# Row maxima turned in 32x32 blocks, context normalised on ScalarE, FFN work re-spaced

## The chip, the cores and the metric

The kernel runs on one core of one Trainium2 chip. The metric is the device time of one execution in microseconds (us): the median of several runs. PE is TensorE, PEld its weight loads, DVE VectorE, ACT ScalarE, POOL GpSimd; SP is SyncE, whose queue issues nearly all transfers (DMAs). A line number such as L836 is a line of the kernel before unless the text says that it is one of the changed kernel.

## What is computed

The input x is 32 sequences of 256 tokens with 128 features, float32. Three residual blocks follow each other:

```python
x = x + 0.5 * ffn(layernorm(x))          # "first FFN"
x = x + attention_block(layernorm(x))    # 16 heads of 8 features
x = x + 0.5 * ffn(layernorm(x))          # "second FFN"
```

The FFN has weights of +1 or -1, made from booleans: 128 to 512 with relu, 512 to 512 with relu, 512 to 128, each with a scale. The attention block projects to Q, K and V, takes a softmax over 256 keys for every head and query, multiplies by V, adds the block's input and ends in a layernorm with gamma and beta.

## The kernel before

**Tiling.** The 32 sequences are worked on as 16 units of two sequences (512 tokens, b = 0 and 1 inside a unit). Activations that enter matmuls are split into two float16 parts, a high one (h1h, h2h, qkhl row 0, xT row 0) and a low one that holds what rounding lost (h1l, h2l and so on), and each weight tile is multiplied with both.

**FFN.** `ffn` runs 4 products for the first layer, 16 for the second (4 outputs, each summed over 4 chunks) and 4 for the third. `dense` (L416) writes each product either as one matmul over all 128 columns of the array (L420, tiling D) or as four that each use 32 columns (L423, tiling C). `relu_split` follows each output: ACT makes the high part, DVE the low part (L664); by choice of the planner ACT instead writes a float32 copy (`full`, L666 or L667) from which POOL casts and subtracts (L661, L667).

**Attention.** For a unit and a sequence, `maxima` runs eight steps: PE makes the scores of two heads' groups (`nat`, L825, with 32 rows of the array each, called tiling R here), and DVE takes the maximum over the keys (`nm`, L836). `shift` turns these maxima into a row that is added to Q's extra rows, so that the second pass over the scores comes out shifted: ACT and POOL split nm into a high and a low float16 part (`mt`, L848 to L850), PE transposes mt into PSUM (`pm`, L855), ACT copies it to SBUF (`mr`, L860), one transfer takes mr to a DRAM tile (`dm`, L861), and another takes dm into the rows of Q (L862). `weigh` runs eight steps again: scores the other way round (`sc`, L895), exp on ACT (`pt`, L907), and products with V (`cx`, L877). `context` transposes cx back (`tp`, L921), divides by the sum of weights, adds the residual, normalises (`normalize`, tag "c") and applies gamma and beta. For all units but the last, `normalize` subtracts the mean and multiplies by the inverse deviation in two POOL operations (L617, L618).

**Order.** Nothing above is issued in the order of its text. Every operation is recorded with an engine, a cost, a due time (`rank`) and what it reads and writes; `_Plan.simulate` then lays all operations out on five engines, lowest rank first, with the buffers that are free, and `run` emits them in that order, which is then fixed on each engine. One step of `maxima` or `weigh` is one unit of rank, called a beat: 16 beats belong to a unit. The first maximum of unit u has rank 16u, and `weigh` follows `maxima` by BW = 13 beats, so that most beats hold one nat and one sc group, which use different rows of the array and are emitted interleaved. Products of the FFN, the projections and the transposes fill the array between the beats. Two PSUM tiles of the tag "sc" hold the scores of both passes, three of the tag "m" hold all other products, pm among them. The first FFN of unit u has due times from B0 + P0*u on (B0 = -30, P0 = 16.003); the second FFN of unit u from B1 + max(16u, 17.354 min(u, 1) + 16 max(u - 1, 0)) on, with B1 = 42.462. `relief` and `divert` in the planner decide, with the constants BIAS and BIAS2, which relu work goes to POOL.

Of the kernel before, what the change touches and what calls it, by code (L numbers as in the profile page):

```python
# [36 lines left out]
F32 = mybir.dt.float32  # L37
F16 = mybir.dt.float16
I32 = mybir.dt.int32
U8 = mybir.dt.uint8  # L40
AF = mybir.ActivationFunctionType
ALU = mybir.AluOpType
AX = mybir.AxisListType

P = 128
H = 16
HD = 8
G = 4
R = 4
EPS = 1e-5  # L50
# [6 lines left out]

QF, QK = 1, 1

QL = 1  # L60

UNIT = 16
B0, BA, BP, BW, BV, B1 = -30, -10.627, -6.547, 13, 4, 42.462

P0, P1, P2, SLOW = 16.003, 17.354, 16, 1

TURN_X, TURN_C = 1.5, 1.5  # L70

WARM = 14

BB = 15.813

RUSH, AHEAD = -0.12, 4.08

SKIP0, SKIP, UNTIL = 10.311, 2.868, 28.215

FAR = 19.64  # L80

HOLD = (0, 0.0, 0.0)

CAST = 1.0

WAIT = 0.057

KIND2 = 'F'

# [2 lines left out]

AFTER, REACH = (0.165, 0.085, 0.11, 0.04, 0.0), (0.053, 0.033, 0.037, 0.08, 0.05)

BIAS = 1.115

BIAS2 = 0.714
PE, DVE, ACT, POOL, SP = range(5)


# [19 lines left out]
class _Plan:  # L120
# [269 lines left out]
def tile_macaron(ctx: ExitStack, tc: tile.TileContext, x, Wq, bq, Wk, bk, Wv, bv, gamma, beta, k0, k1, k2, s0, s1, s2, out):  # L390
    nc = tc.nc
    plan = _Plan(tc)
    op = plan.op
    B, S, D = x.shape
    DFF = k1.shape[0]
    NF = DFF // P
    NU = B // 2
    TU = 2 * S
    NT = TU // P
# [33 lines left out]
    ident16 = const.tile([P, P], F16, name="ident16")  # L433
# [60 lines left out]
    scale = const.tile([P, 3], F32, name="scale")  # L494
# [5 lines left out]
    def projections():  # L500
# [89 lines left out]
    def normalize(dst, src, tag, n, rank, scale=1.0, quick=False):  # L590

        of = lambda: src[0].t[:, src[1] : src[1] + n]
        srcs = [(src[0], src[1] + t) for t in range(0, n, 2)]
        mv = buf(small, [P, n, 2], F32, f"mv{tag}", 4, f"mv_{tag}")
        ve = buf(small, [P, n], F32, f"ve{tag}", 4, f"ve_{tag}")
        rs = buf(small, [P, n, 1], F32, f"rs{tag}", 4, f"rs_{tag}")
        step = 2 if quick else n
        for a in range(0, n, step):
            part = slice(a, a + step)
            ts = range(a, a + step)  # L600
            for t in ts:
                st = buf(small, [P, 6], F32, f"st{tag}", 4, f"st_{tag}_{t}")
                op(DVE, 0.195, lambda t=t, st=st: nc.vector.bn_stats(st.t, of()[:, t, :]), r=[srcs[t // 2]], w=[st], rank=rank)
                op(DVE, 0.085, lambda t=t, st=st: nc.vector.bn_aggr(mv.t[:, t, :], st.t), r=[st], w=[(mv, t)], rank=rank)
            op(POOL, 0.27, lambda part=part: nc.gpsimd.tensor_scalar(ve.t[:, part], mv.t[:, part, 1], EPS, 1.0 / scale**2, ALU.add, ALU.mult),
               r=[(mv, t) for t in ts], w=[(ve, a)], rank=rank)
            op(POOL, 0.35 + 0.2 * step, lambda part=part: nc.gpsimd.tensor_tensor(rs.t[:, part, 0], ve.t[:, part], nhalf[:, part], ALU.pow),
               r=[(ve, a), "nhalf"], w=[(rs, a)], rank=rank)
        mvs = [(mv, t) for t in range(n)]
        if quick:  # L610
            for t in range(n):
                op(DVE, 0.26, lambda t=t: nc.vector.tensor_scalar(dst.t[:, t, :], of()[:, t, :], mv.t[:, t, 0:1], rs.t[:, t, :], ALU.subtract, ALU.mult),
                   r=[srcs[t // 2], (rs, t // 2 * 2), (mv, t)], w=[(dst, t)], rank=rank)
        else:
            dsts = [(dst, t) for t in range(n)]
            cost = 0.2 + 0.2 * n
            op(POOL, cost, lambda: nc.gpsimd.tensor_tensor(dst.t, of(), bc(mv.t[:, :, 0:1], D), ALU.subtract), r=[*srcs, *mvs], w=dsts, rank=rank)  # L617
            op(POOL, cost, lambda: nc.gpsimd.tensor_tensor(dst.t, dst.t, bc(rs.t, D), ALU.mult), r=[(rs, 0)], w=dsts, rank=rank)  # L618
# [19 lines left out]
    xs, xns, xTs, nms, cxs = {}, {}, {}, {}, {}  # L638
# [11 lines left out]
    def norm_ffn(key, src, n, rank, quick):  # L650
        name = f"{key[0][-1]}_{key[1]}_{key[-1]}"
        xn = buf(work, [P, n, D], F32, "fxn", 2, f"fxn{name}")
        normalize(xn, src, f"f{key[0][-1]}", n, rank, XS, quick)
        xTs[key] = turned(xn, key[0][-1], name, n, rank)
# [15 lines left out]
    def ffn(key, srcs, n, rank, span):  # L670
# [49 lines left out]
                0.1 + w / 455, lambda: nc.gpsimd.tensor_tensor(to(), to(), full.t.rearrange("p (t d) -> p t d", d=D), ALU.add)))  # L720
        return dsts

    def norm_first(u):
        norm_ffn(("ffn0", u), (xs[u], 0), NT, (B0 + P0 * u - AHEAD) if u >= QF else B0 - 0.5 + 2 * (u - 1) if u else -950, u < QF)

    def first(u):
        rank = B0 + P0 * u
        ffn(("ffn0", u), (xs[u], 0), NT, rank, P0)

    def second(u, b):  # L730
        n, part = (NT, 0) if b is None else (2, 2 * b)
# [2 lines left out]
        rank = at(u) + (b or 0) * UNIT / 2  # L734
        norm_ffn(("ffn1", u, b), (xs[u], part), n, rank - AHEAD, u >= NU - QL)
        dsts = ffn(("ffn1", u, b), (xs[u], part), n, rank, span * n / NT)
# [103 lines left out]
    def shift(u, b):  # L840

        rank = -1000
        nm, j = nms.pop((u, b)), u % NV
        Q = qs[j]
        nmr = [(nm, g, pr) for g in range(G) for pr in range(2)]
        ns = buf(small, [P, 2, R, G], F32, "ns", 4, f"ns_{u}_{b}")
        mt = buf(small, [P, 2, R, 2, G], F16, "mt", 4, f"mt_{u}_{b}")
        op(ACT, 0.2, lambda: nc.scalar.mul(mt.t[:, :, :, 0, :], nm.t, 1.0 / ONE), r=nmr, w=[(mt, 0)], rank=rank)  # L848
        op(POOL, 0.25, lambda: nc.gpsimd.tensor_scalar(ns.t, nm.t, 1.0 / ONE, None, ALU.mult), r=nmr, w=[ns], rank=rank)
        op(POOL, 0.3, lambda: nc.gpsimd.tensor_tensor(mt.t[:, :, :, 1, :], ns.t, mt.t[:, :, :, 0, :], ALU.subtract), r=[ns, (mt, 0)], w=[(mt, 1)], rank=rank)  # L850
        pm = psum([32, 2, P], f"pm_{u}_{b}", F16)

        def turn():
            for qc in range(2):
                nc.tensor.transpose(pm.t[:, qc, :], mt.t[:, qc].rearrange("p r l g -> p (r l g)"), ident16)  # L855

        op(PE, 0.12, turn, r=[(mt, 0), (mt, 1), "ident16"], w=[pm], rank=(u + 0.5 * b) * UNIT + 8.06, kind="C")
        mr = buf(small, [32, S], F16, "mr", 4, f"mr_{u}_{b}")
        dm = buf(dram, [32, S], F16, "dm", 4, f"dm_{u}_{b}")
        op(ACT, 0.25, lambda: nc.scalar.copy(mr.t, pm.t.rearrange("p q n -> p (q n)")), r=[pm], w=[mr], rank=rank)  # L860
        op(SP, 0.35, lambda: nc.sync.dma_start(out=dm.t, in_=mr.t), r=[mr], w=[dm], rank=rank, lag=1.4)  # L861
        op(SP, 0.63, lambda: nc.sync.dma_start(  # L862
            out=Q.rearrange("(x j) g n -> j x g n", j=16)[3][:, :, b * S : b * S + S],
            in_=dm.t.rearrange("(x g) n -> x g n", g=G)), r=[dm], w=[("S", j, b)], rank=rank, lag=1.8)

    def weigh(u, b):
        base = (u + 0.5 * b) * UNIT + BW
# [85 lines left out]
    for u in range(NU):  # L953
# [48 lines left out]
```

## Time and profile before

| | |
|---|---|
| three runs: median, lowest, highest | 688.74, 687.92, 688.95 us |
| the profiled execution's own time | 689.46 us |
| its span, first to last instruction | 687.6 us |
| mean granted clock of PE over the span | 0.995 |
| busy PE, DVE, ACT, POOL | 659.8, 581.1, 543.1, 497.3 us |
| DMA | 33.59 MB in 33391 packets |

The profile comes from one execution. Its span is 1.86 us shorter than that execution's time; those 1.86 us lie around the program's instructions. A row of a group names the line, the engine, what is written from what, the shape and the count, then busy time and mean duration of one, then the idle time of the engine before such instructions and who ended it. An engine's recorded durations overlap at their edges: DVE's sum to 656 us, of which 581.1 are distinct. Where the text says "exclusive", the time is meant that an instruction adds after the end of the one before it on its engine: 1158 ns for a maximum whose duration is 1216.

### The profile page before, as it was taken

The numbers are of one execution on the slowest core, as the hardware profiler recorded it, in microseconds if no ns is written. First come the engines' busy times: TensorE is split into PE (matmuls) and PEld (weight loads), VectorE is DVE, ScalarE is ACT, GpSimd is POOL, SyncE is SP. The second block draws the span as 40 slices with busy tenths as digits, with TensorE's granted clock in tenths as the row PEclk, the third lists the DMA queues.
The fourth block names the chain that finished last, engine by engine and source line by source line (L and its number), as shares of the span: only waits on it lengthen the run. The fifth ranks groups of instructions, "written<-read, shape, count | busy, mean of one in ns | idle before, by whom it ended". The sixth has DMA issues, their size and how long they took to land.

```text
span 687.6 us, 28926 instructions
## 1 busy us (share of the span) xinstructions
PE 659.8 (96%) x12596; PEld 344.6 (50%) x12596; DVE 581.1 (85%) x1194; ACT 543.1 (79%) x871; POOL 497.3 (72%) x685
## 2 busy tenths in 40 slices
PE   7998978999999999999999999999999999999996
PEld 4544533545455554555455454555445454544455
DVE  7789887998989798898979889897988888889484
ACT  3546887788889888888978888897889787868953
POOL 6875596688686868768686877868686785865643
PEclk9999998999999999999999999999999999999999
DMA  7222200203011030301102030200203021300000
GB/s 222 76 79 80 64 23 3 83 5 98 5 49 54 3 98 4 100 4 58 46 5 97 3 99 5 76 27 16 86 5 97 4 74 30 96 4 20 5 17 31
DMA packets 33391, 33.59 MB, mean 49 GB/s; under 512 B 4992, under 2 KB 29056, under 8 KB 33264
## 3 DMA queue, kind: packets, MB, share of 16 engines
q1 hardware_dynamic: 31520, 30.89, 14.3%
q8 instruction: 99, 1.62, 1.0%
q10 hardware_dynamic: 1744, 0.85, 0.4%
q14 instruction: 28, 0.23, 0.1%
HBM read 18.58 MB, written 13.14 MB: 46 GB/s over the span
## 4 chain that ended last, share of the span: by engine, by line
PE 82%; DVE 7%; ACT 4%; POOL 3%; DMA 2%; issue 1%; SPq 0%; ACTq 0%; POOLq 0%
PE p_None L423 18%; PE p L423 17%; PE cx L877 16%; PE sc L895 9%; PE p L420 6%; DVE nm L836 4%; PE p_None L420 3%; PE nat L825 3%; ACT pt L907 2%; PE tp L921 2%; PE pq L423 2%; PE pq L420 1%; PE pv L423 1%; PE t L630 1%; PE t_None L630 1%
## 5 line engine op out<-in xcount | busy, mean ns | idle before, releaser
L836 DVE TENSOR_REDUCE nm<-nat 128x4 f32<-128x1024 f32 x256 | 310.5, 1216 | 27.4 <-PE nat L825 22.0
L907 ACT ACTIVATE pt<-sc,esc 128x1024 f32<-128x1024 f32 x256 | 285.2, 1116 | 54.7 <-PE nat L825 45.2
L423 PEld LDWEIGHTS <-w 128*32 128x32 f16 x3976 | 97.4, 96 | 102.4 <-issue 28.9
L877 PE MATMUL cx<-pt,vaug 128*32 128x256 f32 x2048 | 137.2, 385 | 0.0
L895 PE MATMUL sc<-qs,ks 32*128 32x256 f16 x1024 | 103.2, 274 | 6.7 <-ACT pt L907 4.9
L825 PE MATMUL nat<-ks,qs 32*128 32x256 f16 x1024 | 101.7, 274 | 3.9 <-ACT pt L907 1.8
L877 PEld LDWEIGHTS cx<-pt,vaug 128*32 128x32 f32 x2048 | 58.6, 110 | 44.7 <-issue 12.3
L423 PE MATMUL p<-h1h,w 128*32 128x512 f16 x796 | 78.5, 383 | 0.0
L423 PE MATMUL p<-h1l,w 128*32 128x512 f16 x796 | 78.0, 380 | 0.0
L423 PE MATMUL p_None<-h1h_None,w 128*32 128x512 f16 x744 | 73.6, 382 | 0.1
L423 PE MATMUL p_None<-h1l_None,w 128*32 128x512 f16 x744 | 73.0, 379 | 0.0
L895 PEld LDWEIGHTS <-ks 32*128 32x128 f16 x1024 | 31.7, 92 | 75.0 <-issue 70.7
L661 POOL TENSOR_TENSOR h2l_None<-full,h2h_None 128x512 f16<-128x512 f32 x27 | 31.5, 1168 | 27.6 <-ACT full L666 27.3
L661 POOL TENSOR_TENSOR h2l<-full,h2h 128x512 f16<-128x512 f32 (+1 forms) x36 | 40.8, 1134 | 11.5 <-ACT full L666 10.8
L663 ACT ACTIVATE h1h<-p 128x512 f16<-128x512 f32 (+1 forms) x68 | 37.3, 577 | 13.6 <-PE p L420 9.0
L825 PEld LDWEIGHTS <-qs 32*128 32x128 f16 x1024 | 31.3, 92 | 29.7 <-issue 28.7
L663 ACT ACTIVATE h2h<-p 128x512 f16<-128x512 f32 (+1 forms) x56 | 32.3, 576 | 15.7 <-PE p L420 11.8
L664 DVE SCALAR_TENSOR_TENSOR h2l_None<-p_None,h2h_None 128x512 f16<-128x512 f32 x33 | 22.7, 687 | 25.7 <-ACT h2h_None L663 25.6
L420 PEld LDWEIGHTS <-w 128*128 128x128 f16 x326 | 30.1, 98 | 28.5 <-issue 10.5
L664 DVE SCALAR_TENSOR_TENSOR h1l<-p,h1h 128x512 f16<-128x512 f32 (+1 forms) x61 | 39.4, 663 | 1.1 <-ACT h1h L663 0.8
L663 ACT ACTIVATE h2h_None<-p_None 128x512 f16<-128x512 f32 x56 | 33.4, 596 | 6.0 <-PE p_None L420 4.9
L423 PE MATMUL p_None<-xT_None,w 128*32 128x512 f16 x480 | 35.4, 380 | 0.0
(163 smaller groups left out, 1471.7 us busy)
## 6 DMA issues: line engine op xcount, KB each, us to landing
dr<-qkhl SPq DMA_DIRECT2D x32, 256.0 KB, 2.0
qs<-dr SPq DMA_DIRECT2D x48, 128.0 KB, 3.3
ks<-dr SPq DMA_DIRECT2D x48, 128.0 KB, 2.6
out_dram<-x SPq DMA_DIRECT2D x15, 256.0 KB, 3.0
x<-in_L_attn_x_dram SPq DMA_DIRECT2D x14, 256.0 KB, 6.1
dm<-mr SPq DMA_DIRECT2D x32, 16.0 KB, 2.5
qs<-dm SPq DMA_DIRECT2D x32, 16.0 KB
qs<-nought SPq DMA_DIRECT2D x13, 32.0 KB
```

Of the source, the lines that this page charges most:

```text
L420: nc.tensor.matmul(to, w, of, start=start, stop=stop)
L423: nc.tensor.matmul(to[32 * r : 32 * r + 32], w[:, 32 * r : 32 * r + 32], of, start=start, stop=stop)
L630: nc.tensor.transpose(pt.t[:, bass.ts(t, P)], xn.t[:, t, :], ident)
L661: return lambda: nc.gpsimd.tensor_tensor(lo.t[:, m, :], of.t, hi.t[:, m, :], ALU.subtract)
L663: h = op(ACT, 0.09 + w / 1280, lambda: nc.scalar.activation(hi.t[:, m, :], ps.t, AF.Relu), r=[ps], w=[(hi, m)], rank=rank)
L664: l = op(DVE, 0.08 + w / 985, lambda: nc.vector.scalar_tensor_tensor(lo.t[:, m, :], ps.t, 0.0, hi.t[:, m, :], ALU.max, ALU.subtract), r=[p ...
L825: nc.tensor.matmul(nat.t[:, ii, qc, :], Q[32 * r : 32 * r + 32, g, b * S + qc * P : b * S + qc * P + P], K[32 * r : 32 * r + 32, g, b * S ...
L836: op(DVE, 1.141, lambda g=g, pr=pr, nat=nat: nc.vector.tensor_reduce(nm.t[:, :, 2 * pr : 2 * pr + 2, g].rearrange("p q i -> p i q"), nat.t ...
L877: nc.tensor.matmul(cx.t[32 * r : 32 * r + 32, g // 2, :], V[:, 2 * b + kc, 4 * (g // 2) + r, 16 * (g % 2) : 16 * (g % 2) + 32], pts[g, r / ...
L895: nc.tensor.matmul(sc.t[:, ii, kc, :], K[32 * r : 32 * r + 32, g, b * S + kc * P : b * S + kc * P + P], Q[32 * r : 32 * r + 32, g, b * S : ...
L907: op(ACT, 1.012, lambda pt=pt, sc=sc: nc.scalar.activation(pt.t, sc.t, AF.Exp, scale=esc), r=[sc, "esc"], w=[pt], rank=rank - RUSH, rush=True)
L921: nc.tensor.transpose(tp.t[:, qc, 8 * c : 8 * c + 8, :].rearrange("p h n -> p (h n)"), cxT.t[:, c, bass.ts(qc, P)], ident)
```

## The change

1. In `shift`, PE's transposes (L855), their PSUM tile and ACT's copy (L860) go. DVE turns mt in 32x32 blocks straight from SBUF to SBUF; each of the four groups of 32 partitions then goes to its place in dm by a transfer of its own, and the transfer from dm to Q waits for all four.
2. `normalize` with the tag "c" (all units but the last): DVE makes one small tile, -mean times inverse deviation, and ACT writes the normalised rows with it as a bias, one instruction for each of the two tiles of 128 tokens. The two POOL operations go.
3. Due times: the first FFNs of units 0 to 6 stand 12 beats apart instead of 16.003, the later ones 18.68 beats. The second FFNs stand 16.954 beats apart up to unit 11, then 11.5, 11.5, 14.5 and 16 beats; B1 is 44.465.
4. Other constants of the planner move: costs it assumes (CAST, one POOL cost), how far it may reach ahead (SKIP0, SKIP, UNTIL, FAR, WAIT, AHEAD), which due time an attention operation has (BA, BP, BB, RUSH, TURN_X), and when relu work goes to POOL (BIAS, BIAS2). No operation is changed by these, only the order and which engine does a relu part.

```diff
+AFFINE = ('c',)
-B0, BA, BP, BW, BV, B1 = -30, -10.627, -6.547, 13, 4, 42.462
-P0, P1, P2, SLOW = 16.003, 17.354, 16, 1
-TURN_X, TURN_C = 1.5, 1.5
+B0, BA, BP, BW, BV, B1 = -30, -10.84, -5.861, 13, 4, 44.465
+P1, P2, SLOW = 16.954, 11.484, 11
+EARLY, COUNT, OVER = 12, 6, 0.101
+TURN_X, TURN_C = 0.5, 1.5
...
-RUSH, AHEAD = -0.12, 4.08
-SKIP0, SKIP, UNTIL = 10.311, 2.868, 28.215
-FAR = 19.64
+RUSH, AHEAD = 0.37, 4.595
+SKIP0, SKIP, UNTIL = 7.606, 3.049, 21.378
+FAR = 11.812
...
-CAST = 1.0
-WAIT = 0.057
+CAST = 0.62
+WAIT = 0.025
...
-BIAS = 1.115
-BIAS2 = 0.714
+BIAS = 1.057
+BIAS2 = 0.73
...
+        elif tag in AFFINE:
+            nb = buf(small, [P, n, 1], F32, f"nb{tag}", 4, f"nb_{tag}")
+            op(DVE, 0.08, lambda: nc.vector.scalar_tensor_tensor(nb.t, mv.t[:, :, 0:1], -1.0, rs.t, ALU.mult, ALU.mult), r=[*mvs, (rs, 0)], w=[nb], rank=rank)
+            for t in range(n):
+                op(ACT, 0.21, lambda t=t: nc.scalar.activation(dst.t[:, t, :], of()[:, t, :], AF.Identity, scale=rs.t[:, t, :], bias=nb.t[:, t, :]),
+                   r=[srcs[t // 2], (rs, 0), nb], w=[(dst, t)], rank=rank)
...
+    def place0(u):
+        rest = ((NU - 1) * UNIT + OVER - EARLY * COUNT) / (NU - 1 - COUNT)
+        return B0 + EARLY * min(u, COUNT) + rest * max(u - COUNT, 0)
...
     def first(u):
-        rank = B0 + P0 * u
-        ffn(("ffn0", u), (xs[u], 0), NT, rank, P0)
+        ffn(("ffn0", u), (xs[u], 0), NT, place0(u), min(UNIT, place0(u + 1) - place0(u)))
...
-        pm = psum([32, 2, P], f"pm_{u}_{b}", F16)
-        def turn():
-            for qc in range(2):
-                nc.tensor.transpose(pm.t[:, qc, :], mt.t[:, qc].rearrange("p r l g -> p (r l g)"), ident16)
-        op(PE, 0.12, turn, r=[(mt, 0), (mt, 1), "ident16"], w=[pm], rank=(u + 0.5 * b) * UNIT + 8.06, kind="C")
-        mr = buf(small, [32, S], F16, "mr", 4, f"mr_{u}_{b}")
+        mr = buf(small, [P, 2, 32], F16, "mr", 4, f"mr_{u}_{b}")
         dm = buf(dram, [32, S], F16, "dm", 4, f"dm_{u}_{b}")
-        op(ACT, 0.25, lambda: nc.scalar.copy(mr.t, pm.t.rearrange("p q n -> p (q n)")), r=[pm], w=[mr], rank=rank)
-        op(SP, 0.35, lambda: nc.sync.dma_start(out=dm.t, in_=mr.t), r=[mr], w=[dm], rank=rank, lag=1.4)
+        op(DVE, 0.14, lambda: nc.vector.transpose(mr.t.rearrange("p q a -> p (q a)"), mt.t.rearrange("p q r l g -> p (q r l g)")), r=[(mt, 0), (mt, 1)], w=[mr], rank=rank)
+        for i in range(4):
+            op(SP, 0.45, lambda i=i: nc.sync.dma_start(out=dm.t.rearrange("x (q i a) -> i x q a", q=2, i=4)[i], in_=mr.t[32 * i : 32 * i + 32]), r=[mr], w=[(dm, i)], rank=rank, lag=1.5)
         op(SP, 0.63, lambda: nc.sync.dma_start(
             out=Q.rearrange("(x j) g n -> j x g n", j=16)[3][:, :, b * S : b * S + S],
-            in_=dm.t.rearrange("(x g) n -> x g n", g=G)), r=[dm], w=[("S", j, b)], rank=rank, lag=1.8)
+            in_=dm.t.rearrange("(x g) n -> x g n", g=G)), r=[(dm, i) for i in range(4)], w=[("S", j, b)], rank=rank, lag=1.8)
```

More of the change, by code (lines that the diff above doesn't have):

```diff
@@ L58 @@
 QF, QK = 1, 1
+AFFINE = ('c',)
 QL = 1
 UNIT = 16
-B0, BA, BP, BW, BV, B1 = -30, -10.627, -6.547, 13, 4, 42.462
-P0, P1, P2, SLOW = 16.003, 17.354, 16, 1
-TURN_X, TURN_C = 1.5, 1.5
+B0, BA, BP, BW, BV, B1 = -30, -10.84, -5.861, 13, 4, 44.465
+P1, P2, SLOW = 16.954, 11.484, 11
+EARLY, COUNT, OVER = 12, 6, 0.101
+TURN_X, TURN_C = 0.5, 1.5
 WARM = 14
-BB = 15.813
-RUSH, AHEAD = -0.12, 4.08
-SKIP0, SKIP, UNTIL = 10.311, 2.868, 28.215
-FAR = 19.64
+BB = 15.721
+RUSH, AHEAD = 0.37, 4.595
+SKIP0, SKIP, UNTIL = 7.606, 3.049, 21.378
+FAR = 11.812
 HOLD = (0, 0.0, 0.0)
-CAST = 1.0
-WAIT = 0.057
+CAST = 0.62
+WAIT = 0.025
 KIND2 = 'F'
@@ L604, in normalize @@
                 op(DVE, 0.085, lambda t=t, st=st: nc.vector.bn_aggr(mv.t[:, t, :], st.t), r=[st], w=[(mv, t)], rank=rank)
-            op(POOL, 0.27, lambda part=part: nc.gpsimd.tensor_scalar(ve.t[:, part], mv.t[:, part, 1], EPS, 1.0 / scale**2, ALU.add, ALU.mult),
+            op(POOL, 0.275, lambda part=part: nc.gpsimd.tensor_scalar(ve.t[:, part], mv.t[:, part, 1], EPS, 1.0 / scale**2, ALU.add, ALU.mult),
                r=[(mv, t) for t in ts], w=[(ve, a)], rank=rank)
@@ L721, in ffn @@
         return dsts
+    def place0(u):
+        rest = ((NU - 1) * UNIT + OVER - EARLY * COUNT) / (NU - 1 - COUNT)
+        return B0 + EARLY * min(u, COUNT) + rest * max(u - COUNT, 0)
     def norm_first(u):
-        norm_ffn(("ffn0", u), (xs[u], 0), NT, (B0 + P0 * u - AHEAD) if u >= QF else B0 - 0.5 + 2 * (u - 1) if u else -950, u < QF)
+        norm_ffn(("ffn0", u), (xs[u], 0), NT, place0(u) - AHEAD if u >= QF else B0 - 0.5 + 2 * (u - 1) if u else -950, u < QF)
     def first(u):
-        rank = B0 + P0 * u
-        ffn(("ffn0", u), (xs[u], 0), NT, rank, P0)
+        ffn(("ffn0", u), (xs[u], 0), NT, place0(u), min(UNIT, place0(u + 1) - place0(u)))
     def second(u, b):
```

## The prediction

> **What bounds the kernel now.** I read the page first, then the same columns for five stretches of the span, then PE's waits in each, then PE's timeline inside the longest. The page, engines and slices:
>
> ```profile
> PE 659.8 (96%) x12596; PEld 344.6 (50%) x12596; DVE 581.1 (85%) x1194; ACT 543.1 (79%) x871; POOL 497.3 (72%) x685
> ...
> PE   7998978999999999999999999999999999999996
> ...
> PEclk9999998999999999999999999999999999999999
> ```
>
> PE is busy nearly always, but "busy" holds pipelined matmuls, so its slack has to be found elsewhere. The stretches (length, then busy time and instructions of PE, PEld, DVE, ACT, POOL, granted clock, DMA) end at the first maximum, after 48 beats, after 224, after 248, and at the end:
>
> ```profile
> 0.00:43.60 43.60, 37.03 (x242) 21.63 (x246) 32.62 (x111) 21.34 (x48) 32.65 (x52) 1.00 0.49 148
> 43.60:137.30 93.70, 84.11 (x1575) 41.37 (x1577) 84.46 (x154) 68.52 (x108) 63.77 (x87) 0.96 0.15 47
> 137.30:575.00 437.70, 437.39 (x9051) 227.10 (x9047) 381.46 (x763) 372.60 (x591) 333.24 (x447) 1.00 0.14 45
> 575.00:624.30 49.30, 45.87 (x892) 23.01 (x888) 42.93 (x81) 38.67 (x57) 37.27 (x55) 1.00 0.12 36
> 624.30:687.60 63.30, 55.44 (x864) 31.48 (x852) 39.63 (x89) 41.93 (x69) 30.32 (x47) 1.00 0.06 20
> ```
>
> Only the third, call it C, is full: PE lacks 0.3 of 437.7 us. In A, B, D and E it lacks 6.6, 9.6, 3.4 and 7.9. PE's timeline in C gives the price of a product:
>
> ```profile
> 240.52 0.39 PE L423 MATMUL p<-h1h,w 128*32 128x512 f16 x4
> 240.74 0.39 PE L423 MATMUL p<-h1l,w 128*32 128x512 f16 x4
> 240.96 0.39 PE L423 MATMUL p<-h1h,w 128*32 128x512 f16 x4
> ```
>
> Four matmuls of tiling C start together and the next four 0.216 us later, though each lasts 0.39. Measured so, start to start: 512 columns 216 ns in tiling C or D, 128 columns 56 ns, a float32 set of cx 216 ns, a float32 transpose 109 ns; a change of tiling adds about 100 ns (216 becomes 320). I call a program's counts times these prices its **stream**. The built order of the kernel before has 572 changes of tiling and a stream of 633.0 us: 30.0, 75.8, 432.8, 42.9 and 51.4 in A to E. In C the measured 437.7 is 1.011 times the stream: C is bound by PE. The other four stretches take 249.9 us for 200.1 of stream; that 49.8 us is what a better spacing can reach.
>
> **The change, part by part.** The built order of the changed kernel, counted alike:
>
> *Turned maxima.* 64 transposes go: 64 x 56 ns = 3.6 us of PE. Changes of tiling become 580: +0.8. The stream becomes 630.2 us, so this part by itself is worth 2.8 us, and ACT loses 32 copies (0.24 us exclusive each, 7.8 us). DVE gains 32 block transposes that the trace does not show: between 84 ns, a bn_aggr's exclusive time, and 381 ns, the multiplication of 256 float32 columns at L934. I take 150, nearer the small one since a row has 64 float16; 4.8 us over the kernel, ends 2.7 and 12.2. In 22 of 32 places the transpose stands behind the first maximum of the next eight (1.16 us), which covers POOL's mt: that ends 0.72 us after the eighth maximum in about half the cases, 1.7 in the others. There DVE now waits some 0.5 us where PE used to wait:
>
> ```profile
> PE pm L855 <- POOL mt L850: 1.6, 3, 1.0
> ...
> PE pm L855 <- ACT full L667: 0.8, 1, 0.8
> ```
>
> What stands behind the DVE transpose is relu parts and the next maximum, for which PE's next scores wait. The four transfers: the one transfer now costs SP 302 to 468 ns and lands after 1.4 to 3.6 us (median 2.5):
>
> ```profile
> L861 SPq DMA_DIRECT2D dm<-mr x32: 302/324/468, 55.2 to 640.7; - x32
> ...
> DMA to landing us min/median/max: 1.4/2.5/3.6
> ```
>
> Three more at 0.32 to 0.65 us (L862's issue) are 1.0 to 2.0 us a row, 31 to 62 us of SP, which already waits 337 us for mr. Behind them on SP stand the transfers of Q, K, x and the output; the row is needed 12.2 us (odd rows, b = 1; 15.4 for even) after the eighth maximum, and its second transfer is issued after 3.4 to 4.9 us (even rows up to 7.1) and needs some 3, as `ks` and `qs` do from `dr`, so the cover holds by 2 us or more except for the last row, whose exp starts after 7.1. There I charge 0.7 us (ends 0 and 2). The Trainium skill ("DMA: Bandwidth & Descriptors", Specifications) wants at least 512 B a piece; the pieces go from 512 to 64 B, which speaks against the change. It gives no price for 16 KB, and the sum does without it.
>
> *Context by ACT.* POOL loses 60 operations of 0.61 us exclusive (36.5 us); ACT gains 60. Their like, 128x128 float32, are rows of 285 (L559) and 392 ns (L547): I take 300, 18 us. DVE gains 30 small ones, 130 to 176 ns by the rows of one to three columns: 160, 4.8 us. None of it is on PE; it lies under C's slack (ACT 372.6, POOL 333.2 of 437.7).
>
> *Relu parts.* The order gives DVE 19 fewer low parts, and POOL 19 more subtractions (1.15 us) and 30 more casts (0.58). In sum DVE 581.1 to 581.1, ACT 543.1 to 545.4, POOL 497.5 to 497.2 us: nothing gained or lost there, only placed.
>
> *Spacing.* This decides. Stream and DVE work in each stretch, before and after:
>
> A: PE 30.0 to 35.2, DVE 32.0 to 33.5. B: PE 75.8 to 85.9, DVE 85.1 to 91.8. C: PE 432.8 to 407.1, DVE 382.6 to 369.5. D: PE 42.9 to 48.7, DVE 42.4 to 45.6. E: PE 51.4 to 53.4, DVE 39.0 to 40.7.
>
> C loses 25.7 us of PE work; A, B, D and E get it where PE has holes. Now the time of each:
>
> A. The second product of Q and K stands 4.0 us later in the stream, and behind it come 8.0 us of products instead of 6.8 before the first scores, which came 9.0 us after it (through `dr`, 2.9 us, and `ks`, 2.7). So 1.2 us less is waited: 35.2 + 13.6 - 1.2 = 47.6.
>
> B. Before, 93.7 is 8.6 over DVE, the largest sum. Part of it is a slower clock:
>
> ```profile
> 102.00:108.00 6.00, 4.59 (x54) 1.91 (x58) 3.99 (x4) 4.01 (x5) 4.15 (x7) 0.61 0.03 7
> 108.00:114.00 6.00, 5.75 (x78) 2.42 (x70) 3.86 (x9) 3.95 (x7) 5.09 (x7) 0.82 0.00 0
> ```
>
> PE was busy for 11.2 us of the 16 before this, with no idle above 1.3 us; then half the clock for 6.8 us, up to 3.4 us lost. The skill ("TensorE: Matmul & The Clock Gate", HAM oscillation) names idle gaps over about 3.4 us as what brings this on; by that rule no gap here is long enough, and the change would win nothing. The trace contradicts the rule, so a fuller PE may win these 3.4 us. The rest of the 8.6 is POOL's queue (the chain of waits runs through POOL from 86 to 102) and beats whose work is uneven. With 91.8 us of DVE: 94.3 if 2.5 of the excess stays, 100.4 if all does. I take 97.0.
>
> C. 407.1 x 1.011 = 411.7. DVE's share rises from 87% to 90%, so I add 1.6 for stalls: 413.3.
>
> D. Before 6.4 over the larger sum; PE now leads DVE by 3.1, so 4.0 stay: 52.7 (ends 49.2 and 55.1).
>
> E. Before 11.9 over the stream, a chain that the change keeps: 53.4 + 11.9 + 0.7 = 66.0.
>
> Sum: 47.6 + 97.0 + 413.3 + 52.7 + 66.0 = 676.6 of span, and 1.86 around it: **678.5 us**, 11.0 under the profiled execution's 689.46 (which is 0.1% over the median of the runs, so the same forecast from the median is 677.8).
>
> **The rivals.** *More than that*: B at 94.3 without the slow clock, C at 409.5 (half of what it now takes over the stream), D at 49.2, the others as above: 47.6 + 94.3 + 409.5 + 49.2 + 66.0 + 1.9 = 668.5; with one of the three missed, 670. For it: C before had no stall at all. Against it: DVE as full as in B.
>
> *Early work given back*: B at 100.4, D at 55.1, and C with 0.05 us of stalls in each of its 176 beats (411.7 + 8.8): 47.6 + 100.4 + 420.5 + 55.1 + 66.0 + 1.9 = 691.5 at the full price, half of the way to it 685. For it: B was never near PE's stream, and POOL has 80.6 us of work in B against 72.5.
>
> *Slower: DVE becomes the bound in C*, because the block transpose waits for POOL's mt at 22 of C's rows and holds the next maximum. Price 0.5 us (1.7 less the 1.16 of cover) to 1.5 us (no maximum ahead, POOL in an operation of 1.2): 11 to 33 us over C's PE time. At 0.5 us a row nothing is left of the gain; at 0.75, 678.5 + 16.5 = 695. Against it: a DVE wait has to outlast PE's own lead, 1.7 us in eight beats, before it counts.
>
> *The change doesn't do what it says* is excluded by the built order, which has no pm and 128 transfers.
>
> **How the numbers follow.** Forecast (674 to 682) 0.50; more (666 to 674) 0.16; given back (682 to 687.3) 0.16; slower 0.12; within 0.2% (1.4 us, about what a measurement of this kernel can tell from no change) 0.06. So faster 0.82, same 0.06, slower 0.12. The range 668 to 690 leaves out about 0.05 below and 0.10 above.
>
> **What would show it.** C shorter by 20 us or more, with PE's waits there under 3 us, confirms the spacing; B 2 to 7 us longer with 10 us more stream confirms DVE as its bound; clock 1.00 throughout B confirms the fuller PE; DVE waits on mt (changed kernel) under 5 us in all rule out the slower rival. The forecast is wrong if C's time per eight beats stays above 19.3 us (425 over 22), or if PE waits on the row of Q fed by dm.

## The result: 0.5% slower, and the profile after

The changed kernel took 692.1 us (median of four runs, 690.84 to 692.62), the kernel before 688.3 us on the same chip: 1.0053 times as long, 95% interval 1.0039 to 1.0067. The forecast was 678.5 us and faster; it was wrong in sign, and the time lies 2.1 us above its range. The profiled execution took 692.19 us with a span of 690.4. Line numbers from here on are those of the kernel that is spoken of.

The page of the changed kernel, its first row of engines, the 40 slices and the clock:

```profile
PE 659.5 (96%) x12559; PEld 338.3 (49%) x12559; DVE 584.3 (85%) x1240; ACT 545.7 (79%) x885; POOL 498.9 (72%) x671
...
PE   7999999999999999989999999999999999989997
...
PEclk9999999999999999999999999999999999999999
```

These rows look better than those of before: the early slices are full and the clock no longer dips. They can't show the loss, because a pipelined matmul counts as busy while the next one is late. The table of the five stretches can, read against each stretch's stream:

```profile
0.00:49.70 49.70, 43.13 (x272) 25.39 (x276) 35.22 (x114) 24.47 (x55) 33.87 (x50) 1.00 0.43 130
49.70:149.00 99.30, 91.97 (x1803) 44.79 (x1795) 90.46 (x184) 76.14 (x122) 76.28 (x101) 1.00 0.15 45
149.00:571.70 422.70, 417.39 (x8539) 209.69 (x8535) 371.09 (x759) 357.27 (x571) 319.71 (x423) 1.00 0.15 46
571.70:625.20 53.50, 49.94 (x1055) 25.13 (x1042) 46.45 (x92) 43.77 (x67) 39.61 (x54) 1.00 0.13 39
625.20:690.40 65.20, 57.08 (x918) 33.32 (x916) 41.11 (x97) 44.01 (x73) 29.43 (x45) 0.99 0.06 19
```

| stretch | stream before, after | time before, after | forecast | missed by |
|---|---|---|---|---|
| A | 30.0, 35.2 | 43.6, 49.7 | 47.6 | 2.1 |
| B | 75.8, 85.9 | 93.7, 99.3 | 97.0 | 2.3 |
| C | 432.8, 407.1 | 437.7, 422.7 | 413.3 | 9.4 |
| D | 42.9, 48.7 | 49.3, 53.5 | 52.7 | 0.8 |
| E | 51.4, 53.4 | 63.3, 65.2 | 66.0 | -0.8 |
| sum | 633.0, 630.2 | 687.6, 690.4 | 676.6 | 13.8 |

A, B, D and E took over 23.1 us of PE's stream and grew by 17.8: there the spacing gained 5.3 us. C gave away 25.7 us of stream and became only 15.0 shorter. What C takes beyond its stream, called its **excess** below, went from 4.9 to 15.6 us. So the question is why C's excess tripled.

PE's waits in C of the changed kernel, the longest first (before, the only one of 0.2 us or more in C was a single wait of 0.2 on DVE):

```profile
PE nat L839 <- DMA ks<-dr: 1.9, 1, 1.9
PE p L427 <- issue: 0.7, 1, 0.7
PE p_None L427 <- issue: 0.6, 1, 0.6
```

These three make 3.2 us. The rest is spread thin: PE's groups in C start later than their prices by more than 40 ns for 11 us in all, against 2.3 before, and some 5 us of the 11 are about 30 short waits for exp, maxima and low parts.

### The profile page after: what moved, and what is told of

Same layout as the page of the kernel before. It is cut to its first block, busy times and chain, and to the rows that moved or that the text cites. A ratio compares the mean times of both kernels' runs of the same rounds, so it can differ in the third digit from the quotient of the medians.

```text
span 690.4 us, 29016 instructions
## 1 busy us (share of the span) xinstructions
PE 659.5 (96%) x12559; PEld 338.3 (49%) x12559; DVE 584.3 (85%) x1240; ACT 545.7 (79%) x885; POOL 498.9 (72%) x671
## 4 chain that ended last, share of the span: by engine, by line
PE 75%; DVE 10%; ACT 9%; issue 3%; DMA 1%; POOL 1%; SPq 0%; ACTq 0%; DVEq 0%; POOLq 0%
PE p_None L427 15%; PE p L427 13%; PE cx L886 13%; PE p L424 8%; PE sc L904 8%; DVE nm L850 4%; ACT pt L916 4%; PE p_None L424 4%; PE nat L839 3%; PE tp L930 2%; PE pq L427 2%; PE ta L640 1%; PE t_None L640 1%; PE t L640 1%; PE pv L427 1%
## 5 line engine op out<-in xcount | busy, mean ns | idle before, releaser
L427 PEld LDWEIGHTS <-w 128*32 128x32 f16 x3464 | 83.1, 96 | 85.7 <-issue 24.9
L427 PE MATMUL p<-h1h,w 128*32 128x512 f16 x640 | 63.1, 382 | 0.1
L427 PE MATMUL p<-h1l,w 128*32 128x512 f16 x640 | 62.6, 379 | 0.0
L424 PEld LDWEIGHTS <-w 128*128 128x128 f16 x454 | 42.5, 98 | 40.1 <-issue 10.8
L948 POOL TENSOR_TENSOR z<-z,gab 128x256 f32<-128x256 f32 x30 | 22.0, 733 | 30.7 <-ACT z L622 30.6
L424 PE MATMUL p<-h1h,w 128*128 128x512 f16 (+1 forms) x128 | 43.7, 353 | 0.4 <-ACT full L677 0.3
L424 PE MATMUL p<-h1l,w 128*128 128x512 f16 (+1 forms) x128 | 43.6, 352 | 0.0
L674 DVE SCALAR_TENSOR_TENSOR h2l<-p,h2h 128x512 f16<-128x512 f32 (+1 forms) x44 | 28.5, 649 | 13.3 <-ACT h2h L673 13.1
L673 ACT ACTIVATE h1h<-p 128x512 f16<-128x512 f32 (+1 forms) x56 | 31.9, 583 | 9.6 <-PE p L424 7.9
L671 POOL TENSOR_TENSOR h2l_None<-full,h2h_None 128x512 f16<-128x512 f32 x27 | 31.5, 1168 | 10.9 <-ACT full L676 10.1
L671 POOL TENSOR_TENSOR h1l<-full,h1h 128x512 f16<-128x512 f32 (+1 forms) x33 | 36.8, 1117 | 3.5 <-ACT full L676 2.7
```

What stands on the lines that cost most here:

```text
L424: nc.tensor.matmul(to, w, of, start=start, stop=stop)
L427: nc.tensor.matmul(to[32 * r : 32 * r + 32], w[:, 32 * r : 32 * r + 32], of, start=start, stop=stop)
L671: return lambda: nc.gpsimd.tensor_tensor(lo.t[:, m, :], of.t, hi.t[:, m, :], ALU.subtract)
L673: h = op(ACT, 0.09 + w / 1280, lambda: nc.scalar.activation(hi.t[:, m, :], ps.t, AF.Relu), r=[ps], w=[(hi, m)], rank=rank)
L674: l = op(DVE, 0.08 + w / 985, lambda: nc.vector.scalar_tensor_tensor(lo.t[:, m, :], ps.t, 0.0, hi.t[:, m, :], ALU.max, ALU.subtract), r=[p ...
L948: op(e, cost, lambda: eng.tensor_tensor(z.t, z.t, gab.unsqueeze(1).broadcast_to([P, 2, D]), ALU.mult), r=["gab"], w=zs, rank=rank)
```

## The experiments

Two kinds are used. "Planned anew" means that an edit is made and the planner lays out the order again. "In the old order" means that every operation keeps its place, cost and due time in the plan, and only what it emits differs. The stretches are marked in each run as they were before. None leaves out work. Intervals are of 95%. Each run's time is a median; its stretches, waits and excess are those of its one profiled execution, which can lie apart from the median (farthest: 697.04 against 692.75 us with the context on POOL, 708.57 against 704.5 with measured costs, 692.07 against 695.13 with the turn planned anew). The granted clock in C was 1.00 in every run, so no excess below is a matter of the clock.

### Undoing one part at a time

The changed kernel with PE's turn and ACT's copy again (parts 2 to 4 stay):

```diff
+        op(PE, 0.12, turn, r=[(mt, 0), (mt, 1), "ident16"], w=[pm], ..., kind="C")
+        op(ACT, 0.25, lambda: nc.scalar.copy(mr.t, ...), r=[pm], w=[mr], rank=rank)
-        op(DVE, 0.14, lambda: nc.vector.transpose(mr.t..., mt.t...), ...)
```

> The changed kernel with the maxima turned by PE and ACT again (ACT context, spacing and constants as changed). Stream by the built order 634.4 us, 4.2 more than the changed kernel, 410.5 of it in C. Theory 'spacing' (shorter, uneven beats leave C's waits without cover): C stays some 15 us over its stream, near 425, and the time rises with the stream to about 696. Theory 'block turn' (four transfers on SP, and DVE waiting for mt, hold C): C falls to 415 to 418, and the time to about 688.

Measured: 703.36 us, ratio 1.0209 (1.0181 to 1.0237), 11.3 us over the changed kernel. 4.2 of it are stream (634.4 against 630.2); C's excess is 19.7. PE's waits show what the block turn does away with:

```profile
PE pm L870 <- DVE qkhl L788: 1.7, 1, 1.7
PE pm L870 <- DVE h1l L674: 1.5, 3, 0.8
```

PE's transposes need one of the three PSUM tiles of tag "m", and stand still until DVE has emptied it. So the block turn is not what made the changed kernel slow. How much of the 11.3 us is the turn's own is not shown, because this order is a new one too.

The changed kernel with the context on POOL again, `AFFINE = ()`:

> The changed kernel with the context normalised by POOL again (block turn, spacing and constants as changed). Stream 629.9 us, 407.5 in C. Theory 'spacing': about 692, C near 423. Theory 'ACT context' (ACT stands waiting for the small DVE tile, and exp behind it; 11 such waits, 6.0 us in C of the changed kernel): C 5 us shorter or more, time 685 to 687.

Measured: 692.75 us, ratio 1.0068 (1.0043 to 1.0092); C's excess 17.1. The profiled execution was the slowest of seven; its clock was 0.98 in B and 0.97 in D. Between these two orders, each laid out for its own operations, ACT's context makes no difference that can be measured.

The changed kernel with the old due times, B1, P0, P1, P2 and SLOW as before, the other constants as changed:

> The changed kernel with the due times of both FFNs as before (block turn, ACT context and the other constants as changed). Stream 630.7 us, 431.3 in C, 99.8 of DVE and PE-bound stretches A and B as before. Theory 'spacing': C at 1.011 to 1.015 of its stream, 436 to 438, and the time about 686 to 687, under before. Theory 'new operations': C about 15 us over the stream, 446, and the time about 696.

Measured: 708.64 us, ratio 1.0281 (1.0248 to 1.0313). A to E: 45.9, 101.2, 442.8, 49.3, 67.4; C's excess 11.5 over a stream of 431.3. Here the row of Q comes late:

```profile
PE sc L900 <- DMA qs<-dm: 4.8, 2, 2.7
```

So with parts 1, 2 and 4 in place, the order with the new due times is 16.5 us faster. Not all of that is spacing: beside the late row, the clock in B was 0.92 (17 us at half the clock), and all four executions had a mean clock of 0.992 or less. Whether they are worth it alone is another question:

### Doing one part at a time, planned anew

The kernel before with parts 1 and 2 (block turn, context on ACT):

> The kernel before with the block turn and the ACT context alone (all due times and constants as before). Stream 631.0 us, 432.1 in C; DVE has 16 us more work than in either kernel, since POOL is given fewer relu parts. Theory 'spacing': C 437 to 439, time 686 to 688. Theory 'new operations': C about 447, time about 697.

Measured: 700.99 us, ratio 1.0169 (1.0139 to 1.02); C's excess 8.6; PE waited 2.4 us for the row of Q.

The kernel before with part 3 alone (the new due times):

> The kernel before with the new due times of both FFNs alone, planned anew (turn, context and all other constants as before). Stream 635.3 us: C 411.9, B 87.7, A 33.9. Theory 'the spacing makes C's waits': C 15 us over its stream, 427, time 694 to 698. Theory 'the spacing is sound and the constants or the operations are at fault': C 417, B near 98, time 684 to 688.

Measured: 709.07 us, ratio 1.0297 (1.028 to 1.0315). A to E: 52.0, 101.1, 435.9, 51.0, 67.0. C's stream fell to 411.9 as in the changed kernel, and its excess rose to 24.0. The same due times lose 20.9 us here and win 16.5 above: the parts don't add up, and a planned order can't be priced by its parts.

### The operations in the old order

The kernel before with the block turn and four transfers, in its old order. PE's operation stays in the plan and emits nothing:

```diff
-        op(PE, 0.12, turn, r=[(mt, 0), (mt, 1), "ident16"], w=[pm], ...)
+        op(PE, 0.12, lambda: None, r=[(mt, 0), (mt, 1), "ident16"], w=[pm], ...)
-        op(ACT, 0.25, lambda: nc.scalar.copy(mr.t, ...), r=[pm], w=[mr], rank=rank)
+        op(ACT, 0.25, lambda: nc.vector.transpose(mr.t..., mt.t...), r=[pm], w=[mr], rank=rank)
-        op(SP, 0.35, lambda: nc.sync.dma_start(out=dm.t, in_=mr.t), ...)
+        op(SP, 0.35, lay, r=[mr], w=[dm], rank=rank, lag=1.4)   # lay: the four transfers
```

> The kernel before with its order kept instruction for instruction, in which only the turning is exchanged: PE's transposes and ACT's copy are left out, and DVE's block transpose and the four transfers stand where the copy and the one transfer stood. Stream 629.0 us (4.0 less), C 430.4. Theory 'order' (the waits in C come from the new plan, not from the new operations): C at 1.011 of its stream, 435, and the time 684 to 686. Theory 'operations' (DVE waiting for mt, or the later row of Q, holds PE): C at 441 or more, time 691 or more, with waits of PE on the row's transfer.

Measured: 691.42 us, ratio 1.0045 (1.003 to 1.006), with a stream of 629.0: 4.0 us less to do and 3.3 us more time; C's excess 6.9.

The same with one transfer for the whole tile instead of four:

```diff
+        op(SP, 0.35, lambda: nc.sync.dma_start(out=dm.t.rearrange("x (q i a) -> i x q a", q=2, i=4), in_=mr.t), ...)
```

> The kernel before in its own order with the block turn, as in the run 'turn in the old order', but with one transfer of the four blocks in place of four. That run was 3.3 us slower than before at 4.0 us less stream; PE waited 3.7 us for the row of Q and 2.8 for K there. Theory 'the four issues on SP are the price' (0.6 us each, 2.4 a row, with the transfers of K behind them): both waits go, time 684 to 686, faster than before. Theory 'the block turn itself or its 64 B pieces are late': the waits for the row stay, time 689 to 692.

Measured: 686.99 us, ratio 0.9975 (0.9964 to 0.9986): faster than the kernel before, and 4.4 us under the run with four. A to E: 44.8, 91.9, 436.9, 48.8, 63.0; C's excess 6.5. PE's waits for transfers, with four,

```profile
PE sc L899 <- DMA qs<-dm: 3.5, 2, 2.9
...
PE nat L825 <- DMA ks<-dr: 2.4, 3, 1.3
```

and all that is left of them with one:

```profile
PE nat L825 <- DMA ks<-dr: 0.8, 2, 0.5
```

The wait for the row of Q is gone, and that for K, whose transfers stand behind on SP, falls to a third. SP's timeline in the changed kernel shows the four issues of one row and, after them, the one that they are for (start, length):

```profile
206.84 2.46 SPq L870 DMA_DIRECT2D dm<-mr  x4
210.53 0.62 SPq L871 DMA_DIRECT2D qs<-dm  x1
```

The four take 2.46 us of SP, a single one of the same 64 B pieces 0.56 (median in the one-transfer run; 0.32 with the 512 B rows of before). Four 4 KB transfers landed after 1.8 us in the median, the one of before after 2.5. So the price lay in the number of issues, but not all 4.4 us are issues: the two profiles differ in B (97.2 against 91.9) and hardly elsewhere, and in B the execution with four also ran 6.8 us at half the clock. Its two executions at a mean clock of 0.998 took 689.3 and 689.6 us, those of the single transfer at 1.00 took 686.7 in the median; 2 to 3 us remain. The rule of the skill weighed in the prediction (512 B a piece) points at the change's transfers, but the pieces are of 64 B in both runs, and the one without the split has no such loss.

The changed kernel in its own order, with one transfer instead of four:

> The changed kernel in its own order, with one transfer of the four 32-partition blocks in place of four (same bytes, same pieces of 64 B). SP issues 96 fewer. If SP's queue is what delays K (2.1 us at 305.8 in the changed kernel) and the row of Q: that wait goes, time 689 to 690. If the four issues are hidden: within 0.2% of the changed kernel, 691 to 693.

Measured: 691.54 us, ratio 1.0046 (1.0029 to 1.0063), A to E 48.6, 100.0, 422.2, 53.5, 65.1, C's excess 15.1. The wait for K fell from 2.2 to 0.3 us over the kernel, but PE's stops without a visible cause (waits put down to "issue") rose from 2.7 to 4.0. The four transfers are not where the 10 us went.

The kernel before with block turn, four transfers and ACT's context in its old order:

> As the run before it, with the context normalised by ACT as well, in the same kept order: the small DVE tile and the two ACT instructions stand where POOL's second operation stood, POOL's two are left out. Stream 629.0 us, C 430.4, ACT 381.1 and DVE 389.5 in C. Theory 'order': 684 to 687. Theory 'operations': ACT's rows wait for the small DVE tile and hold exp; C 5 to 10 us longer than with the turn alone, time 690 to 696.

Measured: 714.38 us, ratio 1.038 (1.0367 to 1.0394), 23 us over the run without the context; C's excess 22.8. ACT's and PE's waits in that run:

```profile
ACT z L629 <- DVE nb_c L627: 18.9, 17, 1.4
```

```profile
PE p_None L423 <- DVE qkhl L789: 8.9, 10, 1.4
```

ACT stands up to 1.4 us for DVE's small tile, 17 times, and all that is queued behind the context rows with it. PE waits ten times for the low part of Q and K on DVE, which needs ACT's high part and frees the PSUM tile of PE's next product; that the one leads to the other is inferred. The queues of ACT and DVE had been laid out without that chain, so the run prices the context in an order that knows nothing of it. An old order prices fairly only what adds no new chain of waits to it.

The changed kernel in its order, with the small tile made by two POOL operations instead of one on DVE:

> The changed kernel in its own order; the small tile of the ACT context is made by two POOL operations instead of one on DVE, at the same place. On DVE it took 0.4 to 1.1 us in 11 of 30 places, each time until a POOL operation that was running had ended; ACT waited 8.6 us for it. Theory 'that wait holds exp and so PE': time 688 to 690, C 419 or less. Theory 'covered': 691 to 693.

Measured: 698.04 us, ratio 1.0142 (1.0122 to 1.0162). ACT's wait for the tile grew from 8.6 us (12 times) to 14.2:

```profile
ACT z L626 <- POOL nb_c L622: 14.2, 15, 1.6
```

### What is it about the order?

*The planner's costs are wrong.* It assumes 0.21 us for an ACT context row that takes 0.41 exclusive, 0.08 for a small tile of 0.16 in the median. The changed kernel planned anew, with the costs that its trace shows:

```diff
-                op(ACT, 0.21, lambda t=t: nc.scalar.activation(dst.t[:, t, :], ...
+                op(ACT, 0.41, lambda t=t: nc.scalar.activation(dst.t[:, t, :], ...
-            op(DVE, 0.08, lambda: nc.vector.scalar_tensor_tensor(nb.t, ...
+            op(DVE, 0.16, lambda: nc.vector.scalar_tensor_tensor(nb.t, ...
...
```

> The changed kernel, planned anew with the costs that its own trace shows in place of the assumed ones (exp 1.055 for 1.012, the ACT context 0.41 for 0.21, the four transfers 0.6 for 0.45, and 16 more). Operations, due times and constants as changed. Stream 630.8 us, 408.3 in C. Theory 'C's waits come from the plan expecting other times than the chip's': C's excess falls from 15.6 to 8 or less, time 682 to 686. Theory 'the waits come from the uneven beats themselves': 690 to 696.

Measured: 704.5 us, ratio 1.0232 (1.0203 to 1.0261); C's excess 20.5. The theory falls: truer costs gave a worse order.

*PE stops inside runs of small matmuls.* PE's timeline of the changed kernel at the first of the two stops without a wait:

```profile
213.88 0.23 PE L427 MATMUL p_None<-w,h2h_None 128*32 128x128 f16 x3
214.75 0.23 PE L427 MATMUL p_None<-w,h2h_None 128*32 128x128 f16 x1 [0.65 <-issue]
```

A group of four breaks after its third matmul for 0.65 us, though the fourth waits for nothing. It stands in a run of third-layer products in tiling C, the first FFN's directly behind the second's, with four weight loads and four matmuls each 56 ns. With the third layer always in tiling D (one load and one matmul instead of four); the same constant also sets the tiling of V's projection and moves the third layer's due times to every second beat:

```diff
-KIND2 = 'F'
+KIND2 = 'D'
```

> The changed kernel with the FFNs' third layer always as one matmul over the whole array (tiling D) in place of four, planned anew: 15889 PE instructions for 21760, stream 632.6 us (2.4 more). In the changed kernel PE stood still 3.7 us without a wait, each time inside third-layer products of both FFNs that follow each other (one instruction per 14 ns). Theory 'PE outruns the loading of its instructions there': such stops vanish, time 690 to 692. Theory 'something else': they stay, time 694.

Measured: 699.87 us, ratio 1.0165 (1.0142 to 1.0189). The stops without a cause went from 2.7 us to none of 0.15 us or more, as expected of them, and C's excess rose to 19.5 all the same: other waits came in (PE for exp 2.3 us, for ACT's `full` 2.0). The matmuls recorded fell from 12559 to 9625. The stops are real, but in C of the changed kernel they make under 2 us, not 10.

*The old order repeats; the new one can't.* Before, the second FFNs are 16 beats apart and the first ones 16.003, so both fall on the same beats of every unit, and PE's sequence is the same from unit to unit (units 4 to 10). At 18.68 and 16.954 beats they drift against the attention, and less than half of PE's sequence in a unit of the changed kernel stands alike in the next. Three runs bear on this. The kernel before with its first FFNs 16.2 beats apart:

```diff
-P0, P1, P2, SLOW = 16.003, 17.354, 16, 1
+P0, P1, P2, SLOW = 16.2, 17.354, 16, 1
```

> The kernel before with the first FFNs 16.2 beats apart in place of 16.003, planned anew; nothing else. PE's sequence in C no longer repeats from unit to unit (50 to 84% alike), the density is that of before: stream 636.3 us, C 432.1. Theory 'repetition' (waits come where the order differs from unit to unit): C's excess 12 us or more, C 444, time 700. Theory 'density': excess 5 to 7, C 438, time 692 to 694.

Measured: 708.28 us, ratio 1.0283 (1.0268 to 1.0299), by an edit of one number. C of this run:

```profile
143.30:591.80 448.50, 442.91 (x8969) 222.64 (x8968) 382.77 (x757) 364.13 (x581) 335.95 (x454) 1.00 0.14 44
```

The stream in C is 432.1, that of before 432.8, so PE has the same work per beat as before and DVE hardly more (382.8 us against 381.5); yet PE lacks 5.6 us now, as it lacks 5.3 in the changed kernel, and the excess is 16.4. Only one due time differs, and with it the order.

The kernel before with its second FFNs one beat later:

```diff
-B0, BA, BP, BW, BV, B1 = -30, -10.627, -6.547, 13, 4, 42.462
+B0, BA, BP, BW, BV, B1 = -30, -10.627, -6.547, 13, 4, 43.462
```

> The kernel before with the second FFNs one beat later (B1 43.462), planned anew; nothing else. The due times repeat every 16 beats, but the order laid out does not (50 to 66% alike). Stream 634.8 us, C 433.2. Theory 'repetition': C's excess 12 or more, 445, time 698 to 702. Theory 'density': 5 to 7, C 439, time 691 to 693. Theory 'any new order fits worse': as 'repetition'.

Measured: 703.61 us, ratio 1.0223 (1.0204 to 1.0241); C's excess 14.3. The spacing is the old one, but PE's sequence came out only some 0.6 alike from unit to unit; it repeats every second unit from unit 5 on. DVE has 17 us more to do in C here (398.5 against 381.5), since POOL was given less.

The changed kernel, with all FFNs 16 beats apart after the first six gaps, so that its order repeats from unit 4 on:

```diff
-P1, P2, SLOW = 16.954, 11.484, 11
+P1, P2, SLOW = 16, 16, 1
-EARLY, COUNT, OVER = 12, 6, 0.101
+EARLY, COUNT, OVER = 12, 6, -24
```

> The changed kernel with its early first FFNs (six gaps of 12 beats), but 16 beats between all later ones and between all second FFNs, so that C repeats (97 to 100% alike from unit 4 to 11). The first FFNs then end 24 beats early, and D has less to fill it. Stream 630.5 us: C 416.9, B 85.9, D 40.5. Theory 'repetition': C's excess 8 or less, C 423 to 425, time 690 (D and E lose some 3). Theory 'density' or 'new operations': C 430 to 433, time 698.

Measured: 718.5 us, ratio 1.0421 (1.0375 to 1.0467); C's excess 35.2, the worst of all. PE's waits from 152 to 596 us:

```profile
PE pq L427 <- issue: 6.6, 13, 0.7
PE nat L839 <- issue: 3.0, 2, 1.7
PE nat L839 <- DMA ks<-dr: 2.2, 2, 1.2
```

A stop without a visible cause at the projection of Q comes once or twice in every unit, 13 times. A repeated order repeats its bad coincidences too; repeating isn't what makes an order good.

The block turn with one transfer, planned anew on the kernel before:

> The kernel before with the block turn and one transfer, planned anew (the run with the same operations in the kept order took 687.0 us, C 436.9 for a stream of 430.4). The new order repeats in C (97 to 100% alike from unit 5 to 11) but is another one; DVE has 400.4 us in C. Stream 631.3, C 431.8. Theory 'repetition': C's excess 5 to 8, 437 to 440, time 687 to 690. Theory 'any new order fits worse': C 443 or more, time 694 or more.

Measured: 695.13 us, ratio 1.0089 (1.006 to 1.0119). The order repeats (0.97 to 1.0 from unit 5 on) and C's excess is 7.5, but its C, 439.3 us, is 2.4 longer than the 436.9 of the same operations in the old order. This profile is of the fastest of four executions; by the medians the new order loses 8.1 us to the old one.

### What the runs say together

| C's excess, us | runs |
|---|---|
| 4.9 to 7.5 | before; turn in old order with four transfers (6.9) and one (6.5); turn planned anew (7.5) |
| 8.6, 11.5 | turn and context planned anew; old due times |
| 14.3 to 24.0 | changed kernel (15.6) and its variants (15.1 to 20.5); 16.2 beats (16.4); other phase (14.3); spacing alone (24.0); ACT's context in the old order (22.8) |
| 35.2 | new parts, repeating |

Shown: (1) C's excess needs no change in what PE and DVE have to do per beat: 16.4 appears with the old work. (2) Taking one suspect away leaves the changed kernel's excess where it was or above: the turn (19.7), the context (17.1), the four transfers (15.1), the planner's assumed costs (20.5), the stops in small matmuls (19.5). (3) The excess goes with the due times of the FFNs. With those of before it is 4.9 to 11.5, in the old order and in three that were planned anew (7.5, 8.6, 11.5); the one exception, 22.8, has ACT's context in queues laid out without it. With other due times it is 14.3 or more in all eleven runs, also where one number was changed and nothing else (16.4, 14.3). In the changed kernel it cost C 10.7 us of the 25.7 that the new due times moved out of it.

Open: how the due times do it, and whether the planner's other constants only fitted the old ones. Repetition alone isn't it. Counting repeats every second unit as well, as in the order with 14.3 and in the one with turn and context (8.6), all excesses under 10 belong to orders that repeat, but so do 14.3, 22.8 and 35.2.

## Why the prediction was wrong, step by step

**The failed step is C**: "407.1 x 1.011 = 411.7. DVE's share rises from 87% to 90%, so I add 1.6 for stalls: 413.3." The 407.1 was right. The factor 1.011 was taken over from a kernel whose order had no stall, as though it were a property of PE's work; it holds for that kernel's due times and order, and no run with other due times came near it. Measured: 15.6 us of excess where 6.2 were allowed, 9.4 of the 13.8 us missed. The reason given for stalls, DVE's share, doesn't size them: the 16.2-beat run has 382.8 us of DVE in 448.5 (85%) and as much excess, the turn planned anew has 399.5 in 439.3 (91%) and 7.5.

**B, A and D** were short by 2.3, 2.1 and 0.8 us. The sign was right: PE's new work there was partly taken into the holes (B: 10.1 us of stream for 5.6 of time). The full clock in B came as expected, 1.00 throughout, but it doesn't confirm that a fuller PE wins it: the slow clock that the profile of before shows was itself the exception. Of 48 executions of that kernel beside the experiments, 36 had a mean clock of 0.999 or 1.00, and the other 12 took 1.5 us longer in the median; of the changed kernel's four, two had 0.996. B grew within the "2 to 7 us" named, so DVE as its bound is consistent, not shown. B's end "100.4 if all stays" was nearly met. In A the wait from Q and K to the first scores did not shrink as I took it to: time over stream is 14.5, before 13.6, taken 12.4. **E** (66.0 against 65.2) was right within 0.8.

**Sizes of the new operations.** The forecast took 300 ns for an ACT context row, 160 for the small tile and 150 for the block turn. The changed kernel's rows (shortest, median and longest ns):

```profile
L622 ACT ACTIVATE z<-y,nb_c,rs_c x60: 477/489/517, 96.1 to 645.3; 128x128 f32<-128x128 f32 x60
L620 DVE SCALAR_TENSOR_TENSOR nb_c<-mv_c,rs_c x30: 129/156/1092, 95.9 to 643.9; 128x2 f32<-128x2 f32 x30
```

Exclusive: 412, 283 in the mean (156 was the median; a third are far longer), and 164 for the turn. That makes ACT 6.7 us and DVE 3.7 us fuller than thought; the runs don't show that it mattered by itself. The issues of dm's pieces, 594 ns, lay at the end of "0.32 to 0.65". "The cover holds by 2 us or more" was right for the order that was built (no wait of PE for the row of Q), wrong in eight other runs with the block turn (3.5 us in the old order; 4.8 and 2.4 with the old due times; 0.6 to 3.1 in five more).

**The rivals.** "DVE becomes the bound", with DVE waiting for POOL's mt, isn't what happened: that wait was 0.7 us, twice in all, well under the 5 us that I named. So the kernel was slower by a mechanism that I had only as a reduced gain: *early work given back* at its full price, 691.5, comes close in every stretch (A 47.6, B 100.4, C 420.5, D 55.1, E 66.0, and 1.9; measured 49.7, 99.3, 422.7, 53.5, 65.2). Its "0.05 us of stalls in each of 176 beats" was 0.06: (15.6 - 4.6) / 176. I counted it with 0.16 and only half of its price, and let its full price, slower than before, carry no chance of its own. **The tests** worked: C shorter by 15.0, not "20 us or more", and 19.2 us for eight beats, hardly under the 19.3 that was named as wrong.

## What to carry to other kernels

Where a list planner fixes the order, the time of a full stretch is its stream plus an excess that belongs to the order and its due times, not to the work: take it from orders laid out with the due times in question (here 14.3 us or more), not from the tuned one (4.9), before crediting a saving smaller than that. Price an operation by putting it into the old order, where its place is kept, if it adds no chain of waits: that showed the block turn with one transfer to be worth 1.4 us (688.34 to 686.99) and the split into four to cost 4.4, some of it by the clock, which the whole change had hidden under 10 us of excess. And an engine that looks 96% busy both before and after says nothing of this; count the stream and subtract.

## What the runs showed of the hardware that was not expected

**DVE's small tile ends with POOL's operation.** At 272 us of the changed kernel, DVE, then POOL (start, length):

```profile
272.20 0.89 DVE L620 SCALAR_TENSOR_TENSOR nb_c<-mv_c,rs_c 128x2 f32<-128x2 f32 x1
```

```profile
271.91 1.16 POOL L671 TENSOR_TENSOR h1l<-full,h1h 128x512 f16<-128x512 f32 x1
```

The tile has two values a row and takes 885 ns; it ends 15 ns after POOL's subtraction. Of the 30 tiles, 19 began with no POOL operation running (in one case 11 ns before its end) and took 129 to 161 ns; the other 11 began inside a POOL tensor_tensor or cast and ended 13 to 17 ns after it, ten of them 410 to 1092 ns long. ACT's context rows wait for it, 8.6 us in all. The Trainium skill ("SBUF — State Buffer", SBUF: two separate sides) says that DVE and GpSimd share a pair of ports, and that a DVE operation with two inputs in SBUF is blocked for the whole of a running GpSimd one that reads SBUF; all 30 tiles agree. DVE's relu parts, of which one input lies in PSUM, were not examined for it.

**Stops of PE without a wait.** Four of 0.2 to 1.2 us in the changed kernel, none in the kernel before, 18 in the run that repeats the changed order, none with the third layer in tiling D. Most stand in or behind third-layer products or projections in tiling C, where PE takes four weight loads and four matmuls every 56 ns (128 columns) or 216 ns (512 columns). All runs together have 49 stops over 0.15 us, and every one ended 1.2 to 1.6 us after an instruction packet of 16 KB had landed, though such packets start 6 us or more apart in the median. The skill ("Runtime: NRT & Kernel Launch", Instruction fetch mechanics) says that instructions are fetched in blocks of 16 KiB and that this is mostly hidden by the pace of issue; the packets agree with the size, and in these 49 places the fetch was not hidden. That PE stood for its next instructions is inferred from this: no run changed the fetching alone.

**The clock.** In the profile of before, PE fell to half the clock for 6.8 us after 16 us at some 70% busy with no idle over 1.3 us. A mean clock as low as in that execution (0.995 or less) stands in 12 of the 48 executions beside the experiments. The changed kernel's profile, with PE fuller there (92.0 of 99.3 us in B), has no such stretch, but two of its four executions had a mean clock of 0.996, so a fuller PE is not shown to prevent it.
